# A four-block transformer on one core: gates, shifts and scales spread over the partitions by transfers through memory instead of matmuls, and a bias added by the vector engine

## The chip, the cores and the metric

The kernel runs on one core of a Trainium2 chip. The core has a matrix engine (TensorE, in the profile PE, its weight loads PEld), a vector engine (DVE), a scalar engine (ACT), a general engine (POOL) and SyncE (SP), which here issues nearly all transfers between memory and the 128 partitions of on-chip memory. Every engine works through its own list of instructions in order and waits on semaphores for the others. The metric is the device time of one execution in microseconds; the time of a kernel is the median of several executions.

## The reference

Four blocks follow one another on x, 4 sequences of 512 tokens with 288 channels, in float32. A vector c (4 x 288), one row per sequence, steers each block:

```python
mod = silu(c) @ w_ada + b_ada                       # 4 x 1728
shift0, scale0, gate0, shift1, scale1, gate1 = split(mod, 6)
h = norm(x) * (1 + scale0) + shift0
x = x + gate0 * (attention(h) @ w_proj + b_proj)    # 16 heads of 18
h = norm(x) * (1 + scale1) + shift1
x = x + gate1 * (gelu(h @ w1 + b1) @ w2 + b2)       # 288 -> 1152 -> 288
```

Block 0 replaces the last line by a mixture of experts: four such products, of which each token takes the two with the largest logits, weighted by their softmax. Blocks 0, 1 and 3 attend over the 512 tokens of a sequence; block 2 attends over the 16 heads within each token. A gate, a shift or a scale is a row of 288 numbers that belongs to a whole sequence, so every token of it needs the same row.

## The kernel before, in words

Tokens lie on the partitions in 16 tiles of 128 (TB = 4 tiles are one sequence). The residual x stays on chip. Attention over tokens is written out in steps (L741): per step the score products (L616) of a group of four heads by one tile, the maxima on DVE (L668), exponentials on ACT (L661), and the products with the values (L690). The queries and keys of the next unit of work are computed by L562, copied, and spread by transfers from qc to the qk buffers (L606). Row maxima travel to qk by small transfers (L680).

The order of the work is not left to a scheduler. A small planner inside the program writes it out: `task(where, due, reads, gen)` puts a generator into one of the lists products, lanes, loads and spreads, with a due time counted in gaps and with the names of what it reads. `gap(us)` is called between the matmuls of the main loop and takes pieces from the lists until the given time is filled; `mark(name, delay)` says from which gap on something counts as finished. `other()` hands out the two or so banks of the accumulation memory that the main loop leaves free, in turn. The order in which the planner writes instructions is each engine's order. So moving one task can shift its neighbours. SP's transfers use eight lanes in turn: a transfer is issued only when the one eight before it has landed.

The steering vectors are made by `modulation` and `mod_product` (L348 to L404): matmuls L358 with silu(c) give rows of four partitions, one per sequence, DVE adds the bias (L364), and for most halves PE transposes shifts and scales (L396) so that they lie along the channels. Three things need a row on all 128 partitions:

- `gating(l, half)` (L406): block l's gate, half 0 for attention and half 1 for the MLP. For each of the four sequences a matmul with K=4 (L413) multiplies a 4 x 128 selector, `selb`, with the four rows, and ACT copies the result to the gate tile (L414). There are eight calls.
- `token_modulation(b)` (L420): shift and scale of block 0's experts, for one sequence; two matmuls (L427) and two ACT operations (L428), the second adding 1 to the scale. There are four calls.
- b2, the second bias of an MLP. `mlp()` (L1590) takes whole sequences: block 3's four, and the first of block 1. It starts each accumulation with a matmul with K=1 (L1625), a row of ones with b2, four per call, then L1628 accumulates the second products and `add_gated` (L518) multiplies by the gate on DVE (L522) and adds to x on POOL (L523). `half_mlp()` (L1653) does the same for half sequences with its own matmuls (L1684).

The selector is loaded by three transfers at the start (L1735), between x and the expert router's weights wg (L1736, L1737). The calls of `gating` and `modulation` are queued in the main program:

Of the kernel before, what the change touches and what calls it, by code (L numbers as in the profile page):

```python
# [10 lines left out]
F32 = mybir.dt.float32  # L11
AF = mybir.ActivationFunctionType
ALU = mybir.AluOpType
# [45 lines left out]
def tile_dit_blocks(ctx: ExitStack, tc: tile.TileContext, x_in, cond_t, sel_den, sel_b, w_gate, layers, out):  # L59
# [33 lines left out]

    products, lanes, loads, spreads = [], [], [], []
    open_product, open_lane, open_load, open_spread = [], [], [], []
    WAIT = "wait"
# [201 lines left out]
    def load_mlp(l, e):  # L298
# [5 lines left out]
        for i in range(NF // 3):  # L304
# [97 lines left out]
    def gate_product(l, half):  # L402
        mod_product(l, half, range(2, 3))
        yield 1.5  # L404

    def gating(l, half):  # L406

        row = rows_of[l, half]
        gate = gates[l, half] = wpool.tile([P, B, C], F32, tag=f"gate{half}", name=f"gate_{l}_{half}")
        at = slice(2 * HP, 2 * HP + B)  # L410
        for b in range(B):
            pg = other()
            nc.tensor.matmul(pg[:, :C], selb[at, b, :], row[at, :C], start=True, stop=True)  # L413
            nc.scalar.copy(gate[:, b, :], pg[:, :C])  # L414
            yield 0.5
        mark(("gate", l, half))

    tokens_mod = {}

    def token_modulation(b):  # L420

        row = rows_of[0, 1]
        tokens_mod[b] = [work.tile([P, C], F32, tag="ho", bufs=2, name=f"mod_{k}_{b}") for k in range(2)]
        for kind in range(2):
            at = slice(kind * HP, kind * HP + B)
            pg = other()
            nc.tensor.matmul(pg[:, :C], selb[at, b, :], row[at, :C], start=True, stop=True)  # L427
# [89 lines left out]

    def add_gated(t0, n, pp, gate, name):  # L518

        b = t0 // TB  # L520
        upd = work.tile([P, 2, C], F32, tag="upd", bufs=2, name=f"upd_{name}")
        nc.vector.tensor_tensor(upd[:, :n, :], pp, gate[:, b : b + 1, :].to_broadcast([P, n, C]), ALU.mult)  # L522
        nc.gpsimd.tensor_tensor(x[:, t0 : t0 + n, :], x[:, t0 : t0 + n, :], upd[:, :n, :], ALU.add)  # L523
# [1018 lines left out]
    def experts(base, start):  # L1542
# [3 lines left out]
        for b in range(B):  # L1546
            due = base + 2 * (LEAD + (b + 1) * NG * TB + 14)
            easy = 80 if b < B - 1 else 0
            task(products, due - 12, [("mod", 0, 1)] + ([("xh", 0, 1, b - 1)] if b else []), token_modulation(b))
            task(lanes, due, [("x", 0, 1, b), ("token mod", b)] + ([("scattered", b - 1)] if b else []), norm(0, 1, b))  # L1550
# [39 lines left out]
    def mlp(l, e, b, groups, hook=None, home="ot"):  # L1590
# [30 lines left out]
        def down(fs, hid):  # L1621
            if fs[0] == 0:
                for t in range(TB):
                    r = slice(t * HP, t * HP + 1)
                    nc.tensor.matmul(banks[:, t, :C], ones[r, :], w["b2"][r, :], start=True, stop=False)  # L1625
            for f, hf in zip(fs, hid):
                for t in range(TB):
                    nc.tensor.matmul(  # L1628
                        banks[:, t, :C], hf[:, t * P : (t + 1) * P], w["w2"][f // 3][:, f % 3, :],
                        start=False, stop=f == NF - 1,  # L1630
                    )
# [4 lines left out]
            if fs[-1] == NF - 1:  # L1636
                for i in range(TB // 2):
                    t0 = b * TB + 2 * i
                    add_gated(t0, 2, banks[:, 2 * i : 2 * i + 2, :C], gate, f"m_{l}_{e}_{b}_{i}")
                    if l == n_layers - 1:  # L1640
# [81 lines left out]
    for b in range(B):  # L1722
# [7 lines left out]
        if b == 2:  # L1730
            for g in range(1, NG):
                w_att[0]["load unit"](g, nc.sync)
            load_modulation(0, 0, range(2, 3))
    for kind in range(3):
        nc.sync.dma_start(selb[kind * HP : kind * HP + B], sel_b)  # L1735
    nc.sync.dma_start(wg[:, :KF, :], w_gate[: KF * P, :].rearrange("(k p) e -> p k e", p=P))  # L1736
# [4 lines left out]
    for l in range(n_layers):  # L1741
# [204 lines left out]
```

## Time and profile before

| | us |
| --- | --- |
| median of 3 executions (2443.11 to 2450.07) | 2448.73 |
| the profiled execution | 2468.24 |
| its span, first to last instruction | 2466.5 |
| PE busy | 2282.2 |
| DVE busy | 1069.5 |
| ACT busy | 832.8 |
| POOL busy | 527.1 |
| mean granted PE clock, share of full speed | 0.941 |

A row of a timeline gives the start, the busy time, the engine, the line of the program, the operation, what it writes and reads, the shape and the number of records in the row; brackets hold the idle time of the engine before the row and what ended it. A float32 matmul has two records on PE. "SPq" is SP's queue of transfers. The row PEclk of the page gives the granted clock of PE in 40 equal slices of the span, in tenths of full speed. The profiled execution is slower than the median by 19.5 us, so differences of a few microseconds between two profiles are to be read stage by stage.

### The profile page before, as it was taken

What the parts mean: (1) busy time and instruction counts of PE and PEld (TensorE: products, weight loads), DVE (VectorE), ACT (ScalarE), POOL (GpSimd) and SP (SyncE); (2) the same over time, 40 slices, a digit from 0 to 9 for tenths busy, and PEclk for the clock granted to TensorE, in tenths of its full rate; (3) what the DMA queues carried; (4) which work ended last, traced back from release to release, by engine and by line L of the source; (5) the groups of instructions that cost most, each with busy time, mean ns of one, the idle gap of its engine ahead of it and who ended that gap; (6) DMA issues with size and microseconds to landing.
All of it is one profiled execution on the core that took longest, in us unless ns stands there. A gap on an engine that the chain in (4) does not pass through costs nothing.

```text
span 2466.5 us, 30142 instructions
## 1 busy us (share of the span) xinstructions
PE 2282.2 (93%) x11188; PEld 1204.9 (49%) x11188; DVE 1069.5 (43%) x1944; ACT 832.8 (34%) x1233; POOL 527.1 (21%) x555
## 2 busy tenths in 40 slices
PE   5999999799998999899998999877799999999998
PEld 2233333257775674333353477655467433333455
DVE  3455665432021014555516457898510455555100
ACT  1344434422221222444425333332233344445311
POOL 2000020221021021100001157888621000001000
PEclk8799999899999998999999999888799799999999
DMA  3221121445553552000100000211110000000000
GB/s 80 70 82 39 44 69 39 106 142 178 174 180 113 169 172 76 15 15 14 31 23 1 23 3 8 59 20 20 33 45 7 22 16 17 15 13 7 1 19 20
DMA packets 163032, 134.22 MB, mean 54 GB/s; under 512 B 81365, under 2 KB 146725, under 8 KB 162886
## 3 DMA queue, kind: packets, MB, share of 16 engines
q1 hardware_dynamic: 159520, 122.39, 17.2%
q0 software_dynamic: 3072, 9.44, 1.2%
q8 instruction: 89, 1.46, 0.2%
q10 hardware_dynamic: 294, 0.47, 0.1%
q14 instruction: 57, 0.47, 0.1%
HBM read 90.67 MB, written 26.25 MB: 47 GB/s over the span
## 4 chain that ended last, share of the span: by engine, by line
PE 80%; DVE 5%; DMA 4%; POOL 3%; ACT 2%; issue 2%; SPq 2%; another core or an unknown queue 0%; ACTq 0%; POOLq 0%; DVEq 0%
PE banks L616 19%; PE banks L562 10%; PE banks L690 7%; PE banks L1477 6%; PE banks L1457 6%; PE banks L727 4%; PE banks L1687 4%; PE banks L1665 4%; PE banks L1628 4%; PE banks L1601 3%; PE banks L840 2%; DMA qk<-qc 2%; POOL pv L876 2%; PE banks L1672 1%; PE banks L508 1%
## 5 line engine op out<-in xcount | busy, mean ns | idle before, releaser
L668 DVE TENSOR_REDUCE mx<-banks 128x1 f32<-128x512 f32 x696 | 448.0, 685 | 373.4 <-PE banks L616 370.6
L616 PE MATMUL banks<-qk 32*128 32x512 f32 x3072 | 548.5, 678 | 26.2 <-DMA qk<-qc 13.6
L661 ACT ACTIVATE ex<-banks 128x1024 f32<-128x1024 f32 x348 | 356.4, 1024 | 511.0 <-PE banks L616 506.9
L616 PEld LDWEIGHTS banks<-qk 32*128 32x128 f32 x3072 | 176.6, 193 | 245.0 <-DVE mx L668 96.5
L690 PE MATMUL banks<-ex,va 128*32 128x512 f32 x1536 | 213.2, 626 | 0.0
L562 PE MATMUL banks<-ht,wqk 96*128 96x512 f32 (+1 forms) x360 | 195.1, 649 | 8.7 <-POOL wqk L284 8.1
L876 POOL TENSOR_TENSOR pv<-hs,qk 128x1152 f32<-128x1152 f32 x60 | 190.1, 3182 | 23.3 <-ACT hs L1017 23.3
L1477 PE MATMUL banks<-w_b,hid_b 128*128 128x288 f32 x684 | 188.2, 417 | 0.0
L1457 PE MATMUL banks<-block,w_b 128*128 128x256 f32 x684 | 166.0, 388 | 3.8 <-DMA w_b<-in_w 2.8
L710 POOL COPY rec<-r 128x512 f32<-128x512 f32 x48 | 29.6, 617 | 642.8 <-DVE r L706 569.1
L1469 ACT ACTIVATE hid_b<-banks,b_b 128x256 f32<-128x256 f32 x171 | 68.8, 473 | 247.9 <-PE banks L1463 150.8
L1477 PEld LDWEIGHTS banks<-w_b,hid_b 128*128 128x128 f32 x684 | 124.3, 191 | 51.9 <-issue 24.8
L1665 PE MATMUL banks<-ht,w 128*128 128x256 f32 x504 | 131.9, 397 | 18.8 <-ACT hid L1676 18.3
L1457 PEld LDWEIGHTS banks<-block,w_b 128*128 128x128 f32 x684 | 129.6, 194 | 30.0 <-issue 9.2
L1687 PE MATMUL banks<-w,hid 128*128 128x288 f32 x504 | 144.2, 421 | 0.0
L727 PE MATMUL banks<-wp,ot 128*128 128x288 f32 x384 | 120.4, 440 | 5.9 <-DVE upd_a L522 3.5
L1665 PEld LDWEIGHTS banks<-ht,w 128*128 128x128 f32 x504 | 97.3, 198 | 42.7 <-ACT hid L1676 21.5
L523 POOL TENSOR_TENSOR x<-x,upd_a 128x288 f32<-128x288 f32 x48 | 38.1, 794 | 370.5 <-DVE upd_a L522 347.9
L562 PEld LDWEIGHTS banks<-ht,wqk 96*128 96x128 f32 (+1 forms) x360 | 62.1, 194 | 110.3 <-issue 87.6
L1687 PEld LDWEIGHTS banks<-w,hid 128*128 128x128 f32 x504 | 89.4, 189 | 43.0 <-issue 24.7
L727 PEld LDWEIGHTS banks<-wp,ot 128*128 128x128 f32 x384 | 69.2, 196 | 77.1 <-issue 52.6
L690 PEld LDWEIGHTS banks<-ex,va 128*32 128x32 f32 x1536 | 31.2, 110 | 153.2 <-issue 151.5
(226 smaller groups left out, 2564.6 us busy)
## 6 DMA issues: line engine op xcount, KB each, us to landing
w_b<-in_w SPq DMA_DIRECT2D x57, 432.0 KB
w_b<-in_w SPq DMA_DIRECT2D x57, 384.0 KB
qk<-qc SPq DMA_DIRECT2D x327, 38.0 KB
wa<-in_wada SPq DMA_DIRECT2D x7, 864.0 KB
block<-x_mem SPq DMA_DIRECT2D x19, 288.0 KB
y_mem<-y_b SPq DMA_DIRECT2D x19, 288.0 KB
x_mem<-zeros SPq DMA_DIRECT2D x7, 768.0 KB
y_mem<-zeros SPq DMA_DIRECT2D x7, 768.0 KB
```

What stands on the lines that cost most here:

```text
L562: nc.tensor.matmul(to, st(rows, k), mv(rows, k), start=k == 0, stop=k == NK - 1)
L616: nc.tensor.matmul(to, qk[u][r, of, c * P : (c + 1) * P], qk[u][r, 1 - of, :], start=True, stop=True)
L661: nc.scalar.activation(e, WEIGHTS, AF.Exp)
L668: nc.vector.tensor_reduce(mxs[mu % 2][:, mc, h : h + 1], pm[j], AX.X, ALU.max)
L690: nc.tensor.matmul(SUMS[j * HP : (j + 1) * HP, :], vas[0][:, c, at : at + HP], ex[step, j // 2][:, j % 2, :], start=c == 0, stop=c == TB - 1,)
L727: nc.tensor.matmul(pp, done[b * NG + g][:, t * P : (t + 1) * P], w["wp"][:, g, :], start=g == 0, stop=g == NG - 1)
L876: engine.tensor_tensor(prod, sc[i][:, hs, :].unsqueeze(2).to_broadcast([P, GH, HD, NH]), qkv[i][:, 1].rearrange("p h d -> p d h").unsqueez ...
L1457: nc.tensor.matmul(banks[:, UP + j, :BT], w1[:, k, j * P : (j + 1) * P], hx[i][:, k, :], start=k == 0, stop=False)
L1477: nc.tensor.matmul(banks[:, PY + t, :C], hid[j][:, t * P : (t + 1) * P], w2[:, j, :], start=f == 0, stop=f == NF - 1)
L1628: nc.tensor.matmul(banks[:, t, :C], hf[:, t * P : (t + 1) * P], w["w2"][f // 3][:, f % 3, :], start=False, stop=f == NF - 1,)
L1665: nc.tensor.matmul(banks[:, UP + j, :BT], full[:, k, (f % 3) * P : (f % 3 + 1) * P], h[:, k, s], start=k == 0, stop=False,)
L1687: nc.tensor.matmul(banks[:, PY + t, :C], hf[:, t * P : (t + 1) * P], w["w2"][f // 3][:, f % 3, :], start=False, stop=f == NF - 1,)
```

## The change

`gating` no longer uses PE and ACT. It writes its four rows to memory by a transfer, lets four gaps pass, and reads them back by one transfer that gives each of the 128 partitions all four rows (589,824 bytes written on chip). `token_modulation` does the same with one row of shift and one of scale, each written once as four rows and read per sequence; 1 is added to the scale once, by DVE, on the four rows. These tasks stand in a list of their own, `casts`. The first gate waits in the plan for the maxima of unit 2 also. `mlp()` loads b2 onto all partitions by one transfer, and `add_gated` adds it on DVE ahead of the gate. `half_mlp()` is unchanged. The selector and its three loads are gone.

```diff
+        fill(casts, open_cast, 1000.0)
...
-    selb = const.tile([P, B, P], F32, name="selb")
...
-                for r in range(TB):
-                    nc.sync.dma_start(t["b2"][r * HP : r * HP + 1, :], w["b2"][e : e + 1, :])
+                nc.sync.dma_start(t["b2"], w["b2"][e : e + 1, :].to_broadcast([P, C]))
...
         if (l, half) == (0, 1):
-            mark(("mod", l, half), 2)
+            scale = rows_of[l, half][HP : HP + B, :C]
+            nc.vector.tensor_scalar_add(scale, scale, 1.0)
+            yield 1.0
+            tokens_mod["rows"] = [to_memory(rows_of[l, half][k * HP : k * HP + B, :C], f"t{k}") for k in range(2)]
+            mark(("mod", l, half), 6)
             return
...
+    def to_memory(row, name):
+
+        mem = dram.tile([row.shape[0], C], F32, tag="row", bufs=4, name=f"row_mem_{name}")
+        nc.sync.dma_start(mem, row)
+        return mem
+
     def gating(l, half):
-        row = rows_of[l, half]
+        mem = to_memory(rows_of[l, half][2 * HP : 2 * HP + B, :C], f"{l}_{half}")
+        for _ in range(4):
+            yield WAIT
         gate = gates[l, half] = wpool.tile([P, B, C], F32, tag=f"gate{half}", name=f"gate_{l}_{half}")
-        at = slice(2 * HP, 2 * HP + B)
-        for b in range(B):
-            pg = other()
-            nc.tensor.matmul(pg[:, :C], selb[at, b, :], row[at, :C], start=True, stop=True)
-            nc.scalar.copy(gate[:, b, :], pg[:, :C])
-            yield 0.5
-        mark(("gate", l, half))
+        nc.sync.dma_start(
+            gate.rearrange("p b c -> p (b c)"), mem.rearrange("(o b) c -> o (b c)", o=1).to_broadcast([P, B * C])
+        )
+        mark(("gate", l, half), 8)
+        yield 0.0
...
     def token_modulation(b):
         for kind in range(2):
-            at = slice(kind * HP, kind * HP + B)
-            pg = other()
-            nc.tensor.matmul(pg[:, :C], selb[at, b, :], row[at, :C], start=True, stop=True)
-            nc.scalar.activation(tokens_mod[b][kind], pg[:, :C], AF.Copy, bias=float(kind))
-            yield 0.5
-        mark(("token mod", b))
+            nc.sync.dma_start(tokens_mod[b][kind], tokens_mod["rows"][kind][b : b + 1, :].to_broadcast([P, C]))
+        mark(("token mod", b), 8)
+        yield 0.0
...
-    def add_gated(t0, n, pp, gate, name):
+    def add_gated(t0, n, pp, gate, name, bias=None):
+        if bias is not None:
+            nc.vector.tensor_tensor(upd[:, :n, :], pp, bias.unsqueeze(1).to_broadcast([P, n, C]), ALU.add)
+            pp = upd[:, :n, :]
         nc.vector.tensor_tensor(upd[:, :n, :], pp, gate[:, b : b + 1, :].to_broadcast([P, n, C]), ALU.mult)
...
         def down(fs, hid):
-            if fs[0] == 0:
-                for t in range(TB):
-                    r = slice(t * HP, t * HP + 1)
-                    nc.tensor.matmul(banks[:, t, :C], ones[r, :], w["b2"][r, :], start=True, stop=False)
...
-                        start=False, stop=f == NF - 1,
+                        start=f == 0, stop=f == NF - 1,
...
-    for kind in range(3):
-        nc.sync.dma_start(selb[kind * HP : kind * HP + B], sel_b)
...
-        task(products, base + 20, [("gate row", l, 0)] + before, gating(l, 0))
+        task(casts, base + 20, [("gate row", l, 0)] + before + ([("maxima", 0, 2)] if l == 0 else []), gating(l, 0))
...
-        task(products, base + 60, [("gate row", l, 1)] + before, gating(l, 1))
+        task(casts, base + 60, [("gate row", l, 1)] + before, gating(l, 1))
```

In the order that the planner writes, the modulation tasks (1,0), (3,0) and (3,1) come a little later than before, since they wait for a gate's mark; modulation (1,1) comes earlier; and one piece of block 0's key and query products (L562, second sequence, fourth tile group) comes about five steps later.

More of the change, by code (lines that the diff above doesn't have):

```diff
@@ L92, in tile_dit_blocks @@
     ready = {}
-    products, lanes, loads, spreads = [], [], [], []
-    open_product, open_lane, open_load, open_spread = [], [], [], []
+    products, lanes, loads, spreads, casts = [], [], [], [], []
+    open_product, open_lane, open_load, open_spread, open_cast = [], [], [], [], []
     WAIT = "wait"
@@ L404, in gate_product @@
         yield 1.5
+    def to_memory(row, name):
+        mem = dram.tile([row.shape[0], C], F32, tag="row", bufs=4, name=f"row_mem_{name}")
+        nc.sync.dma_start(mem, row)
+        return mem
     def gating(l, half):
-        row = rows_of[l, half]
+        mem = to_memory(rows_of[l, half][2 * HP : 2 * HP + B, :C], f"{l}_{half}")
+        for _ in range(4):
+            yield WAIT
         gate = gates[l, half] = wpool.tile([P, B, C], F32, tag=f"gate{half}", name=f"gate_{l}_{half}")
-        at = slice(2 * HP, 2 * HP + B)
-        for b in range(B):
-            pg = other()
-            nc.tensor.matmul(pg[:, :C], selb[at, b, :], row[at, :C], start=True, stop=True)
-            nc.scalar.copy(gate[:, b, :], pg[:, :C])
-            yield 0.5
-        mark(("gate", l, half))
+        nc.sync.dma_start(
[3 more added lines that the diff above has]
+        yield 0.0
     tokens_mod = {}
     def token_modulation(b):
-        row = rows_of[0, 1]
         tokens_mod[b] = [work.tile([P, C], F32, tag="ho", bufs=2, name=f"mod_{k}_{b}") for k in range(2)]
         for kind in range(2):
-            at = slice(kind * HP, kind * HP + B)
-            pg = other()
-            nc.tensor.matmul(pg[:, :C], selb[at, b, :], row[at, :C], start=True, stop=True)
-            nc.scalar.activation(tokens_mod[b][kind], pg[:, :C], AF.Copy, bias=float(kind))
-            yield 0.5
-        mark(("token mod", b))
+            nc.sync.dma_start(tokens_mod[b][kind], tokens_mod["rows"][kind][b : b + 1, :].to_broadcast([P, C]))
+        mark(("token mod", b), 8)
+        yield 0.0
     xh, ht = {}, {}
@@ L1548, in experts @@
             easy = 80 if b < B - 1 else 0
-            task(products, due - 12, [("mod", 0, 1)] + ([("xh", 0, 1, b - 1)] if b else []), token_modulation(b))
+            task(casts, due - 12, [("mod", 0, 1)] + ([("xh", 0, 1, b - 1)] if b else []), token_modulation(b))
             task(lanes, due, [("x", 0, 1, b), ("token mod", b)] + ([("scattered", b - 1)] if b else []), norm(0, 1, b))
@@ L1638, in down @@
                     t0 = b * TB + 2 * i
-                    add_gated(t0, 2, banks[:, 2 * i : 2 * i + 2, :C], gate, f"m_{l}_{e}_{b}_{i}")
+                    add_gated(t0, 2, banks[:, 2 * i : 2 * i + 2, :C], gate, f"m_{l}_{e}_{b}_{i}", w["b2"])
                     if l == n_layers - 1:
```

## The prediction

> **What bounds the kernel now.** I read the page's first rows, then the chain.
>
> ```profile
> PE 2282.2 (93%) x11188; PEld 1204.9 (49%) x11188; DVE 1069.5 (43%) x1944; ACT 832.8 (34%) x1233; POOL 527.1 (21%) x555
> ...
> PEclk8799999899999998999999999888799799999999
> ...
> PE 80%; DVE 5%; DMA 4%; POOL 3%; ACT 2%; issue 2%; SPq 2%; another core or an unknown queue 0%; ACTq 0%; POOLq 0%; DVEq 0%
> ```
>
> TensorE (PE) is busy 93% of the span and holds 80% of the chain that ended last. So a matmul taken from a stretch where PE has no gaps shortens the end by its length, and one taken from a stretch held by another engine is worth less. The timeline of PE shows which removed matmul lies where. First the start, PE and then SP's queue:
>
> ```profile
> 46.33 2.04 PE L616 MATMUL banks<-qk 32*128 32x512 f32 x2 [12.54 <-DMA qk<-qc]
> 49.44 2.20 PE L616 MATMUL banks<-qk 32*128 32x512 f32 x6 [1.07 <-DMA qk<-qc]
> ...
> 72.84 3.06 PE L413 MATMUL banks<-row,selb 4*128 4x288 f32 x8
> ```
> ```profile
> 31.34 6.82 SPq L1735 DMA_DIRECT2D selb<-in_sel_b  x3
> 38.20 0.57 SPq L1736 DMA_DIRECT2D wg<-in_w_gate  x1
> 38.82 0.46 SPq L1737 DMA_DIRECT2D wg<-in_w_gate  x1
> 39.40 21.55 SPq L606 DMA_DIRECT2D qk<-qc  x13
> ```
>
> PE waits 12.54 us for the first spread of the queries (L606), and SP issues it only after the three selb loads, of which the second waits 6 us for a DMA lane. Then gates inside other work (one matmul is two records):
>
> ```profile
> 119.05 0.51 PE L427 MATMUL banks<-row,selb 4*128 4x288 f32 x1
> 119.06 0.92 PE L616 MATMUL banks<-qk 32*128 32x512 f32 x3
> ...
> 489.53 1.59 PE L427 MATMUL banks<-row,selb 4*128 4x288 f32 x4 [0.25 <-ACT block L1431]
> ...
> 1024.78 1.23 PE L616 MATMUL banks<-qk 32*128 32x512 f32 x3 [3.34 <-DVE mx L668]
> 1024.80 1.32 PE L413 MATMUL banks<-row,selb 4*128 4x288 f32 x2
> ...
> 1403.15 2.47 PE L413 MATMUL banks<-row,selb 4*128 4x288 f32 x8
> ...
> 1581.92 1.36 PE L413 MATMUL banks<-row,selb 4*128 4x288 f32 x4
> 1586.59 2.28 PE L413 MATMUL banks<-row,selb 4*128 4x288 f32 x4 [3.31 <-ACT gate L414]
> ...
> 1835.18 2.52 PE L413 MATMUL banks<-row,selb 4*128 4x288 f32 x8
> ```
>
> The windows by stage show where PE is no bound: from 1600 to 1750 it is busy 108.8 of 150 us, POOL 115.6, DVE 120.1. From 120 to 300 it is busy 176.4 of 180.
>
> **The change part by part**, against the profiled span of 2466.5 us.
>
> *Start.* Without selb, wg's first load issues at 31.3, its second takes the lane wait to 37.5, and the first spreads go out at 38.0 to 39.9 instead of 39.4 to 42.9: 3.0 us. PE then runs without gaps from 49.4, so 3.0 comes through (0 if the spreads wait for lanes anyway, 4 if not at all).
>
> *Gates (L413), eight calls.* Each loses four matmuls. In full-clock stretches without gaps a call is 2.4 to 2.5: (2,0) 2.4, (3,0) 2.4, (1,0) between the rows of 507 and 513 2.4. (0,0) lies at half clock, 3.0. (0,1) and (1,1) are mixed in pairs with L616, which the K=4 matmul overlaps: 2.0 each. (3,1) at 1928 lies in a stretch where L631's maxima on DVE hold PE: 1.0 (0 to 2.5). (2,1) takes away 3.31 of idle and 3.3 of matmuls, but in front of the stretch that POOL and DVE hold: 3.3 (0 to 11.9, below).
>
> The Trainium skill, "TensorE: Matmul & The Clock Gate", Part 1: an idle window of about 3.4 us puts PE at half clock, and as much sustained work gives full clock back. The first half agrees with the 3.31 us row. The second doesn't: the window 1584 to 1607 has clock 0.50 for 23 us with PE 17.2 busy. By the rule the cure would be worth 3.3 + 1.7 = 5.0 us, by the row up to 3.3 + 8.6 = 11.9. I take neither in full, since POOL is busy 18.7 and DVE 20.0 of those 23 us: PE's slowness is mostly hidden there.
>
> *Token modulation (L427), four calls.* By the periods of the neighbouring L616 rows a matmul costs 0.43 to 0.48, not its 0.9 of busy: six in the first three calls (b = 0 to 2) 2.9; the last call 1.5 at half clock. 4.4.
>
> *Moves.* modulation(1,1) (L358, L364, L396) comes earlier. Its POOL copies (L366) stand ahead of the scatter of b=2 in POOL's order, and in the trace the scatter starts at 518.5 although its places are ready at 508.4; about 3 us earlier then. An idle of 2.89 us before L396 at 530.6 goes or shrinks. I take 2.0 (-1 to 4). qc of b=1, m=4 (L562) moves five steps of 5.2 us later; its spread needs a qk buffer that is free only two steps before the move ends and is used five steps after (26 us, of which nine transfers take up to 18): 8 us of margin, so nothing.
>
> *b2 (L1625), five calls.* The page has 40 records of 0.40, 16 us. But the group of L1628 with them has a period of 12.72 us, without them 12.23: [...] 0.49 x 5 = 2.4.
>
> *What is added.* DVE: ten adds like this row of the tail, 0.76 each:
>
> ```profile
> 2456.82 0.76 DVE L522 TENSOR_TENSOR upd_m<-banks,gate 128x576 f32<-128x576 f32 x1 [29.04 <-PE banks L1628]
> 2457.66 2.75 POOL L523 TENSOR_TENSOR x<-x,upd_m 128x576 f32<-128x576 f32 x2 [28.00 <-DVE upd_m L522]
> 2457.79 0.76 DVE L522 TENSOR_TENSOR upd_m<-banks,gate 128x576 f32<-128x576 f32 x1 [0.21 <-PE banks L1628]
> ```
>
> At the very end the order is add, multiply, add, multiply, so POOL's second L523 starts after four operations instead of two; POOL's first hides part: +1.1. In layer 1's early call the add precedes waiting L616 products: +0.8. The other calls hide it: DVE is idle 28 us before them; bare, they would cost 1.5 each. DVE's scale+1 (one 4x288) hides behind the maxima.
>
> *Transfers*, all in SP's order, eight DMA lanes in turn: 8 writes and 8 broadcasts of 576 KB (gates), 2 writes and 8 broadcasts of 144 KB (token modulation); less 3 selb and 9 of b2. An issue occupies SP 0.25 to 0.6. A write must have landed before its broadcast issues. The trace has no 576 KB broadcast; the nearest rows are rows<-scratch (L906, 576 KB) landing after 3.9 to 4.8, and b_b<-in_b (L1416, one row to 128 partitions, 144 KB) after 2.3 to 4.8. So 4 to 19 (four times the slower), I take 5, nearest to the equal size. The skill speaks against this part: "DMA: Bandwidth & Descriptors", section "Anatomy of one DMA": each transfer has about 2 us of fixed cost, mostly the write's receipt, heaviest towards HBM. By it the round trip costs at least 4; the trace says more, 5.3 to 7.9 for scratch<-ho (L902, to memory) plus 4.8, some 11. Either would be lost if anything waited. But SP's next urgent issues are further off: after gate (0,0), (1,0), (1,1), (3,1), these are due about 9, 12, 11 and 12 us after the broadcast issues (an estimate: gate (1,1) can issue near 1041, since its write follows POOL's combine that ends at 1027, and the next maxima issue near 1052; gate (1,0) near 527, w1's products start at 539); the other gates have 20 and more; the gates themselves are read tens of us later. The waiting instruction is SP's broadcast (for its write), and behind it in SP's order stand: at (0,0) the zeros of x_mem (768 KB) and unit 2's or 3's maxima; at (1,0) the next expert's w1; at (1,1) and (3,1) the next maxima (L680); at token modulation b=0, with gate (0,1), the spread of unit 4, issued at 118 to 124 and used near 150. In attention the write before qk's third spread puts eight instead of six of its nine issues behind the 864 KB wa load's lane, +1.3 us, against 27 us until its products. So 0.
>
> *ACT* loses 40 copies, off the path but for (2,1).
>
> *Sum:* 3.0 + gates (3.0 + 2.0 + 2.4 + 2.0 + 2.4 + 3.3 + 2.4 + 1.0 = 18.5) + 4.4 + 2.0 + 2.4 = 30.3; less 1.9 = 28.4. The profiled execution goes from 2468.2 to about 2440. It lies 19.5 above the median; the same microseconds off the median give 2448.7 - 28.4 = **2420**. Its own range, with low and high ends mixed: 2406 to 2436.
>
> **Rivals.**
> - *More than the sum.* With the stall at 1583 the 23 us of half clock go, and other stalls move off the edge of the clock: +8.6 there, 3 more at 530, and one half-clock stretch of 10 us (as at 1024 to 1034, 4.6 in excess): -45, 2404. For it: PEclk is at 7 and 8 in ten slices. Against: POOL and DVE hold 1600 to 1750.
> - *It doesn't do what it says.* The short K=4 and K=1 matmuls lie beside others in the array, as b2's do, and only start and the solid runs at 72, 489, 1403 and 1835 count (3.0 + 3.0 + 1.5 + 4.8 - 1.9 = 10.4): 2438; with the start hidden too, 2441. Against: the L413 rows at 1403 and 1835 are blocks of eight with nothing in between.
> - *Slower.* One memory row read by 128 partitions is slow, 19 us. Then what SP issues next is late by 10, 7, 8 and 7 us at the four gates named, and each stall brings half clock, 4.6 in excess as at 1024: 32 + 18 = 50, less 28: +22, 2471. From about 13 us per broadcast it decides. For it: 128 reads of one row in one memory. Against: the b_b row.
>
> **How the numbers follow.** Forecast 0.66, more 0.12, little 0.09, slower 0.13. This kernel's measurement tells about 0.3%, 7.3 us: faster is below 2441.4. The forecast and the larger gain are faster, 0.78; with the upper half of "little", 0.80; same 0.08; slower 0.12. The range leaves out most of "slower" and the tip of "more": 2404 to 2445.
>
> **What would show it.** PE with 120 records fewer than 11188 (64 of L413, 16 of L427, 40 of L1625) and busy about 26 us less than 2282.2 (gates 18.5 less the 3.3 of idle, 4.4, 2.4, and some 4 that lay beside L616); first L616 near 43; no idle near 1583; gate<- broadcasts landing in 4 to 6 us; no new wait of L616 on qk<-qc or qk<-maxima; a tail one microsecond longer. The prediction is wrong if L616 or L1457 shows new idle ended by DMA above 5 us, or if the half-clock stretches shift: one more of 23 us costs up to 9.

## The result

The changed kernel takes 2428.6 us (median of 7 executions, 2424.1 to 2436.3), the kernel before 2448.7 (7 executions beside it, 2442.7 to 2456.7). The ratio is 0.9917, 95% interval 0.9898 to 0.9937: 20 us faster, where 28 were forecast. A second set of executions on another occasion (run e8_after) gave the same ratio, 0.9917 (0.9900 to 0.9935). The profiled execution took 2431.8 us, its span is 2430.1.

The page of the changed kernel, the rows that answer to those shown of before:

```profile
PE 2234.5 (92%) x11068; PEld 1186.2 (49%) x11068; DVE 1079.8 (44%) x1955; ACT 818.6 (34%) x1193; POOL 527.0 (22%) x555
...
PEclk8999999899999998999999999897899799999999
...
PE 78%; DVE 6%; DMA 5%; POOL 4%; SPq 3%; ACT 2%; issue 2%; POOLq 0%; ACTq 0%; DVEq 0%
```

PE has the 120 records less that were counted, and is still the bound. Lines have moved: L616 is now L624, L1628 is L1632.

The first profile of the kernel before was a long execution (2468 us), so its difference of 36 us to the one above isn't the change's worth. I profiled the kernel before a second time (run e9_before, 2442.8 us, a short one) and cut the three spans at the same matmuls. Windows of that second profile of before; the columns are the stretch and its length, busy time of PE, PEld, DVE, ACT and POOL with their instructions, granted PE clock, DMA share and GB/s:

```profile
59.14:111.66 52.52, 50.24 (x212) 17.04 (x212) 26.05 (x43) 18.09 (x27) 1.42 (x2) 0.83 0.25 80
111.66:281.65 169.99, 166.36 (x1005) 60.02 (x1001) 98.70 (x183) 78.91 (x92) 8.48 (x14) 1.00 0.16 58
281.65:441.31 159.66, 153.54 (x902) 58.88 (x901) 102.25 (x253) 70.43 (x84) 32.79 (x53) 1.00 0.17 55
441.31:516.74 75.43, 60.31 (x291) 36.20 (x288) 20.84 (x96) 20.42 (x38) 15.43 (x28) 0.84 0.49 142
...
1254.56:1414.55 159.99, 146.27 (x734) 78.47 (x733) 84.22 (x143) 61.95 (x86) 31.01 (x33) 0.95 0.03 10
...
1544.59:1614.58 69.99, 54.44 (x203) 35.76 (x201) 62.71 (x78) 21.94 (x40) 62.64 (x44) 0.77 0.13 23
...
1764.61:1824.61 60.00, 59.94 (x264) 41.22 (x263) 6.19 (x19) 22.63 (x45) 13.03 (x20) 1.00 0.15 46
```

The same stretches of work in the changed kernel:

```profile
60.77:110.47 49.70, 42.98 (x192) 13.82 (x194) 26.97 (x46) 15.07 (x18) 1.42 (x2) 0.93 0.38 103
110.47:282.39 171.92, 167.26 (x1002) 61.69 (x999) 98.10 (x182) 78.55 (x90) 8.82 (x14) 1.00 0.18 62
282.39:447.75 165.36, 157.33 (x894) 58.26 (x893) 102.45 (x253) 68.91 (x80) 32.70 (x53) 0.97 0.17 55
447.75:516.00 68.25, 53.75 (x279) 34.04 (x276) 20.38 (x96) 18.23 (x32) 15.43 (x28) 0.85 0.58 169
...
1251.96:1407.60 155.64, 139.86 (x726) 75.77 (x725) 86.89 (x145) 60.44 (x82) 31.48 (x33) 0.96 0.04 14
...
1537.60:1606.67 69.07, 47.00 (x195) 32.88 (x193) 63.44 (x79) 20.80 (x36) 63.54 (x44) 0.83 0.15 33
...
1757.37:1814.72 57.35, 57.35 (x256) 39.99 (x255) 6.19 (x19) 21.05 (x41) 13.03 (x20) 1.00 0.18 59
```

The stretches where the clock stays at 1.00 have the same length in every profile of one kernel to 0.1 us, so this comparison is sharp there. It shows at once that the third stretch, with token modulation in it, became 5.7 us *longer*, and that where PE got lighter in the sixth (54.4 to 47.0 busy) the stretch became only 0.9 shorter. The table sets the prediction's terms beside it. "Before" is the second profile and, for the first rows, where the clock differs from execution to execution, also the first profile and that of run e3_bias, which is the kernel before up to the middle; "after" is the two profiles of the changed kernel.

| stage of the first profile (us) | what the sum held there | forecast | measured |
| --- | --- | --- | --- |
| 0 to 60 | start | -3.0 | PE's wait 12.54 to 12.18: -0.4 |
| 60 to 120 | gates (0,0), (0,1), token b=0 | -5.9 | 52.5 to 60.0 becomes 47.2 and 49.7: about -8, between -3 and -13, nearly all of it clock |
| 120 to 290 | nothing | 0 | +1.9 (0.9 of PE work in another order, with less beside it, and 1.1 of idle; e1_gates has it too) |
| 290 to 460 | token b=1, b=2 | -1.9 | 159.7 becomes 163.7 and 165.4: +4 to +6 |
| 460 to 540 | token b=3, gate (1,0), the moves | -5.9 | -7.3 |
| 1000 to 1050 | gate (1,1) | -2.0 | -0.8 |
| 1050 to 1280 | b2 of the first call | -0.5 | -0.5 |
| 1280 to 1440 | gate (2,0), the early call's adds | -1.6 | -4.4 |
| 1570 to 1640 | gate (2,1) | -3.3 | -0.9 |
| 1790 to 1850 | gate (3,0) | -2.4 | -2.7 |
| 1850 to 1960 | gate (3,1) | -1.0 | -0.6 |
| 2280 to the end | b2, four calls, and the tail | -0.9 | +0.1 |

The stages left out together give about -1, and with them the measured column sums to some -20, as the medians do.

The start, first PE and then SP's queue of the changed kernel:

```profile
48.10 2.04 PE L624 MATMUL banks<-qk 32*128 32x512 f32 x2 [12.18 <-DMA qk<-qc]
```
```profile
30.43 0.38 SPq L1738 DMA_DIRECT2D wg<-in_w_gate  x1
39.69 0.33 SPq L1739 DMA_DIRECT2D wg<-in_w_gate  x1
40.14 22.52 SPq L614 DMA_DIRECT2D qk<-qc  x13
```

The wait for a lane that selb's second load had is now wg's second load's, as forecast, and the first spread is issued 0.5 us after the lane comes free and not 2. Yet PE waits 12.18 us and not 9.5. (In this execution the start as a whole is 2 us late, from the loads ahead.)

The end of the changed kernel:

```profile
2418.26 0.76 DVE L528 TENSOR_TENSOR upd_m<-banks,b 128x576 f32<-128x576 f32 x1 [26.63 <-PE banks L1632]
2419.05 0.76 DVE L530 TENSOR_TENSOR upd_m<-upd_m,gate 128x576 f32<-128x576 f32 x1
2419.73 0.75 DVE L528 TENSOR_TENSOR upd_m<-banks,b 128x576 f32<-128x576 f32 x1
2419.96 1.40 POOL L531 TENSOR_TENSOR x<-x,upd_m 128x576 f32<-128x576 f32 x1 [26.85 <-DVE upd_m L530]
2420.51 1.45 DVE L530 TENSOR_TENSOR upd_m<-upd_m,gate 128x576 f32<-128x576 f32 x1
2422.11 1.40 POOL L531 TENSOR_TENSOR x<-x,upd_m 128x576 f32<-128x576 f32 x1 [0.76 <-DVE upd_m L530]
```

Four operations stand on DVE as expected; the last multiply, which now reads upd and no longer the accumulation banks, takes 1.45 and not 0.76 while POOL's add runs; the first one takes 0.76 with POOL at rest.

### The profile page after: what moved, and what is told of

It is laid out like the page before. It is cut to its first block, busy times and chain, and to the rows that moved or that the text cites. A ratio compares the mean times of both kernels' runs of the same rounds, so it can differ in the third digit from the quotient of the medians.

```text
span 2430.1 us, 29899 instructions
## 1 busy us (share of the span) xinstructions
PE 2234.5 (92%) x11068; PEld 1186.2 (49%) x11068; DVE 1079.8 (44%) x1955; ACT 818.6 (34%) x1193; POOL 527.0 (22%) x555
## 4 chain that ended last, share of the span: by engine, by line
PE 78%; DVE 6%; DMA 5%; POOL 4%; SPq 3%; ACT 2%; issue 2%; POOLq 0%; ACTq 0%; DVEq 0%
PE banks L624 19%; PE banks L570 9%; PE banks L698 7%; PE banks L1485 7%; PE banks L1465 6%; PE banks L735 4%; PE banks L1691 4%; PE banks L1669 4%; PE banks L1632 4%; PE banks L1609 3%; POOL pv L884 2%; DMA qk<-qc 2%; PE banks L848 2%; PE banks L1676 1%; DVE mx L676 1%
## 5 line engine op out<-in xcount | busy, mean ns | idle before, releaser
L624 PE MATMUL banks<-qk 32*128 32x512 f32 x3072 | 540.2, 668 | 30.3 <-DMA qk<-qc 13.2
L624 PEld LDWEIGHTS banks<-qk 32*128 32x128 f32 x3072 | 174.5, 190 | 256.4 <-DVE mx L676 101.7
L1691 PEld LDWEIGHTS banks<-w,hid 128*128 128x128 f32 x504 | 90.6, 191 | 43.6 <-issue 24.7
L735 PEld LDWEIGHTS banks<-wp,ot 128*128 128x128 f32 x384 | 67.9, 193 | 77.9 <-issue 54.4
```

The lines of the kernel that those rows point to most:

```text
L624: nc.tensor.matmul(to, qk[u][r, of, c * P : (c + 1) * P], qk[u][r, 1 - of, :], start=True, stop=True)
L735: nc.tensor.matmul(pp, done[b * NG + g][:, t * P : (t + 1) * P], w["wp"][:, g, :], start=g == 0, stop=g == NG - 1)
L1691: nc.tensor.matmul(banks[:, PY + t, :C], hf[:, t * P : (t + 1) * P], w["w2"][f // 3][:, f % 3, :], start=False, stop=f == NF - 1,)
```

## The experiments

My theory after the result: the removed lengths are as read, but PE's clock and the waits that the short matmuls used to fill decide as much as the lengths do. The rivals: lengths alone, and a payback through SP's queue. To weigh the clock I use PE's busy time times (1 - granted clock), summed over windows of one microsecond, and call it the excess over full speed: 107.7 and 88.5 us in the two profiles of before, 76.1 and 74.2 in the two of after.

### The three parts alone (e1_gates, e2_tokens, e3_bias)

Each is the kernel before with one part of the diff. e1_gates:

```diff
-            nc.tensor.matmul(pg[:, :C], selb[at, b, :], row[at, :C], start=True, stop=True)
-            nc.scalar.copy(gate[:, b, :], pg[:, :C])
+        nc.sync.dma_start(
+            gate.rearrange("p b c -> p (b c)"), mem.rearrange("(o b) c -> o (b c)", o=1).to_broadcast([P, B * C])
+        )
```

> The kernel before with only the eight gates moved to transfers through memory (selector and its loads kept for the token modulation). Theory by the sum: the removed L413 matmuls give about 18 us and modulation moves may give 2 more, none of the 3.0 of the start: 2428 to 2432 if the sum's terms hold, and L624-type waits on qk transfers stay as before. Rival, the clock: half-clock stretches fall differently, so the time lies up to 12 us away from that either way, while the full-clock stretches show only the matmuls' own lengths. Rival, payback: if SP's queue pays back, a new wait of the score products on DMA appears and the time is above 2438.

Measured: 2437.1 (7 executions), ratio 0.9954 (0.9938 to 0.9970), 11 us faster, less than the sum's 18 or 20.

e2_tokens:

```diff
-            nc.tensor.matmul(pg[:, :C], selb[at, b, :], row[at, :C], start=True, stop=True)
-            nc.scalar.activation(tokens_mod[b][kind], pg[:, :C], AF.Copy, bias=float(kind))
+            nc.sync.dma_start(tokens_mod[b][kind], tokens_mod["rows"][kind][b : b + 1, :].to_broadcast([P, C]))
```

> The kernel before with only the token modulation moved to transfers through memory. Theory by the sum: 4.4 us, so about 2444. Rival, the clock: within 3 us of before or past 8 us, with the difference in half-clock stretches. Rival, payback: slower than before, with qk spreads late after 118 us.

Measured: 2455.9 (14 executions), ratio 1.0024 (1.0011 to 1.0036): slower by 6 to 7.5 us, where a gain of 4.4 was expected. The theory of lengths falls for this part. It was run again later as e12_tokens:

> The kernel with only the token modulation through memory once more, unaltered, beside the one before it in the list (K=4 against K=128) on the same chip. 2454 to 2458 if the first measurement holds, with the half-clock stretch near 492 to 514 again.

Measured: 2453.1 (12 executions), ratio 1.0013 (0.9995 to 1.0030): slower or equal, no gain.

It is lost at two places. The first: the stage of token modulation b=1 and b=2 (290 to 460) is 159.7 us long in e1_gates, in e3_bias and in the second profile of before, which keep L427, and 163.7 to 165.5 in ten profiles of kernels without it. (The first profile of before is the exception: 170.0, with 8.5 of excess there.) Around token modulation b=2, the timeline of the second profile of before:

```profile
389.05 0.66 PE L717 MATMUL banks<-ident,rec 128*128 128x128 f32 x4
389.64 0.51 PE L427 MATMUL banks<-row,selb 4*128 4x288 f32 x1
...
390.23 1.02 PE L616 MATMUL banks<-qk 32*128 32x512 f32 x3
391.75 1.69 PE L616 MATMUL banks<-qk 32*128 32x512 f32 x4 [0.51 <-DMA qk<-maxima]
393.38 1.06 PE L690 MATMUL banks<-ex,va 128*32 128x512 f32 x8
```

and of the changed kernel:

```profile
392.41 0.66 PE L725 MATMUL banks<-ident,rec 128*128 128x128 f32 x4
393.00 1.37 PE L624 MATMUL banks<-qk 32*128 32x512 f32 x4
395.12 1.82 PE L624 MATMUL banks<-qk 32*128 32x512 f32 x4 [0.75 <-DMA qk<-maxima]
396.87 1.94 PE L698 MATMUL banks<-ex,va 128*32 128x512 f32 x8
```

PE reaches the wait for the row maxima sooner, since L427 no longer stands in front of it; the wait grows from 0.51 to 0.75 us, and the next products run at half speed (1.94 us for 1.06). The maxima themselves are not later: the products behind the wait start 2.70 us after the row of L717 (391.75 and 389.05) and 2.71 after that of L725 (395.12 and 392.41), so the broadcasts that now share SP's queue didn't hold them up here. The two or three such stretches cost 3.4 to 5.1 us of excess, and idle grows by 1.9, against 1.3 us of matmuls saved. That the longer wait sets off the half clock is read from the order of these rows and not shown: no run changed the wait alone, the first profile of before had half clock after a wait of 0.50 at 405.6 too, and longer waits in the same stage (1.94 us in the second profile of before, 1.77 in the changed kernel) were not followed by it, though one of 1.78 in e2_tokens was.

The second place: from 460 to 540, where gate (1,0) still stands as K=4 matmuls, e2_tokens takes 80.8 us and e12_tokens 82.5, for 75.4 in the second profile of before; excess is 14.2 and 15.2 for 7.6. The section on e11_gate128 comes back to it.

e3_bias:

```diff
-                    nc.tensor.matmul(banks[:, t, :C], ones[r, :], w["b2"][r, :], start=True, stop=False)
+            nc.vector.tensor_tensor(upd[:, :n, :], pp, bias.unsqueeze(1).to_broadcast([P, n, C]), ALU.add)
```

> The kernel before with only b2 added by DVE in the whole-sequence MLPs. Theory by the sum: 2.4 gained, 1.9 given back: 0.5 us, 2448. By the matmuls' busy time (16 us) it would be 2435. If the tail costs more than 1.1 (the profile of the changed kernel suggests 2.1), 2449; the order of PE is otherwise untouched, so every full-clock stretch ahead of 1260 us must agree to 0.1 us and any difference there is the clock alone.

Measured: 2451.2 (14 executions), ratio 1.0008 (0.9994 to 1.0022): no difference, as expected. Per call PE comes 0.48 to 0.52 us earlier; from PE's last matmul to the end it is 1.7 us longer (10.51 for 8.86).

### The selector's loads put back (e4_selb)

```diff
+    for kind in range(3):
+        nc.sync.dma_start(selb[kind * HP : kind * HP + B], sel_b)
```

> The changed kernel with the three selector loads put back at their place (the tile is loaded and not used). Theory by the sum: 3.0 us slower than the changed kernel, 2431 to 2432, with the first spreads issued some 1.5 to 3 us later after the lane's release. Rival: the start is held by the lane and the landing of the spread, the loads only fill the wait: equal to the changed kernel, 2428 to 2429.

Measured: 2433.6 (6 executions), ratio 0.9927 (0.9908 to 0.9947), which the time can't tell from the changed kernel (the median lies 3 to 5 us above that kernel's two, the intervals overlap). The trace can: PE's wait is 12.55 us with the loads and 12.18 without, 0.4 and not 3.0. The landings say why. In the first profile of before four spreads issued at 39.4, 41.3, 42.0 and 42.9 land at 44.6, 46.2, 47.8 and 49.3; in the second profile of the changed kernel four spreads issued at 38.3, 39.0, 39.6 and 40.3 land at 44.5, 46.1, 47.6 and 49.2. Spreads land one every 1.55 us, whenever they are issued: earlier issue only makes the flight longer (6.3 to 8.9 us and not 4.9 to 6.4). From the release of the lane to the first landing it is 7.0 us in both profiles of before and 6.7 in both of the changed kernel, although the first spread is issued 1.4 us sooner after that release. The rival holds; what sets the first landing stays open.

### Extra matmuls: K=4 against K=128 (e5_k4, e6_k128)

The changed kernel, with 32 matmuls that nobody reads at the places where the gates' stood. K is the number of rows (partitions) over which a matmul sums, of 128. Both kernels have the same order on PE and differ in K alone:

```diff
+        task(products, base + 20, [("gate row", l, 0)] + before, extra_products(l, 0))
...
+        at = slice(2 * HP, 2 * HP + B)
...
+            nc.tensor.matmul(pg[:, :C], ident[at, :], extra[at, :], start=True, stop=True)
```

In the second kernel `at` is slice(0, P), all 128 rows.

> The changed kernel with 32 extra matmuls at the eight places in the plan where the gates' matmuls stood, K=4 like those, of the same length, on constants; nobody reads them and no copy follows. Theory of lengths: they cost what the sum took for the gates, 15 to 18 us, so about 2445, with as much PE time at half clock as in the changed kernel (76 us in excess of full speed in its profile). Rival, the clock counts rows: matmuls that use 4 of 128 rows look like idleness to PE's clock gate, so excess at half clock rises by 10 to 20 and the time is about 2455, at or above the kernel before.

> The same as the run before it, in the same order on every engine, with K=128 in place of K=4. Theory of lengths: the same 2445, or up to 3 more because K=128 can't lie beside the 32-row score products. Rival, the clock counts rows: excess at half clock stays at 70 to 80, the time is 2443 to 2448 and lies 8 or more under the run with K=4.

Measured: with K=4 2453.4 (12 executions), ratio to before 1.0019 (1.0001 to 1.0038); with K=128 2443.0 (7 executions), 0.9958 (0.9940 to 0.9977). One record lasts 0.40 us in both. The 10 us between them aren't length: excess is 93.2 with K=4, 78.5 with K=128, and the mean granted clock of every execution is 0.939 to 0.951 with K=4 (12 executions) and 0.952 to 0.957 with K=128 (7). The stage of the first two gates (60 to 120), with K=4:

```profile
58.86:118.76 59.90, 57.08 (x210) 18.46 (x210) 26.64 (x45) 15.06 (x18) 1.42 (x2) 0.72 0.29 86
```

and with K=128:

```profile
58.84:112.40 53.56, 50.75 (x209) 17.27 (x210) 27.17 (x46) 15.09 (x18) 1.42 (x2) 0.84 0.25 80
```

These two rows alone prove little, since this stage ran from 52 to 60 us in profiles of one kernel, the one before; the times and the clocks of all executions carry the reading. So a matmul on 4 of 128 rows costs its length and, in this stream, a lower clock besides. (K=4 also lay beside other matmuls more: the work that it adds over run e8_after, busy less excess, is 12 us, with K=128 16.)

### The gates on PE, but with K=128 (e11_gate128)

e2_tokens, its 32 gate matmuls made K=128 by a selector that is zero outside four rows:

```diff
-            nc.tensor.matmul(pg[:, :C], selb[at, b, :], row[at, :C], start=True, stop=True)
+            nc.tensor.matmul(pg[:, :C], selb[:, b, :], row[:, :C], start=True, stop=True)
```

> The kernel with only the token modulation through memory and the gates by matmuls, but those 32 matmuls with K=128 in place of K=4: the selector is zero outside its four rows and the rows' tile is cleared before it is filled (nine short DVE memsets more, two selector loads fewer); order on PE the same. If PE's clock counts rows: 8 to 12 us less than the same kernel with K=4, some 2445, and no half-clock stretch of 20 us at the first expert block near 490 to 515. Rival, lengths alone: 2455 to 2458, K=128 not being shorter.

Measured: 2438.2 (6 executions), ratio 0.9948 (0.9931 to 0.9965), against 2453.1 for e12_tokens on the same chip: 15 us, by filling rows with zeros. The mean granted clock is 0.952 to 0.959 in these 6 executions, 0.941 to 0.949 in the 12 of e12_tokens. Gate (1,0) in e12_tokens, timeline and then windows:

```profile
501.55 1.13 PE L1464 MATMUL banks<-block,w_b 128*128 128x256 f32 x4 [0.55 <-ACT hid_b L1476]
502.61 0.86 PE L424 MATMUL banks<-row,selb 4*128 4x288 f32 x2
503.39 2.08 PE L1464 MATMUL banks<-block,w_b 128*128 128x256 f32 x4
505.40 1.32 PE L424 MATMUL banks<-row,selb 4*128 4x288 f32 x2
```
```profile
502.00:524.00 22.00, 22.00 (x64) 10.94 (x63) 4.55 (x22) 2.92 (x8) 2.71 (x6) 0.53 0.15 49
```

and in e11_gate128:

```profile
488.79 1.13 PE L1467 MATMUL banks<-block,w_b 128*128 128x256 f32 x4 [0.55 <-ACT hid_b L1479]
489.75 0.65 PE L427 MATMUL banks<-row,selb 128*128 128x288 f32 x2
490.24 1.03 PE L1467 MATMUL banks<-block,w_b 128*128 128x256 f32 x4
```
```profile
480.00:502.00 22.00, 21.45 (x116) 15.37 (x115) 8.61 (x39) 4.00 (x10) 5.52 (x9) 1.00 0.21 67
```

With K=4 the clock is 1.00 up to 503 and 0.50 from 504 to 523: it falls during the first K=4 row, and from 504 to 523 PE is busy for all 19.00 us. With K=128 it stays at 1.00 after the same wait of 0.55. The whole stage, first in e12_tokens, then in e11_gate128:

```profile
457.89:540.39 82.50, 66.58 (x287) 38.60 (x284) 20.62 (x96) 19.70 (x36) 15.44 (x28) 0.77 0.47 138
```
```profile
445.79:516.87 71.08, 56.93 (x287) 35.70 (x284) 21.46 (x98) 19.80 (x36) 15.43 (x28) 0.86 0.53 156
```

It isn't certain each time: both profiles of the kernel with only the token part have this stretch (that of e12_tokens is one of its longer executions, 2466.5 us, that of e2_tokens, 2455.1, is not), but in the two profiles of before and in e3_bias the same K=4 gate at this place ran at full clock.

### Broadcasts four times as long (e10_slow)

```diff
+        for _ in range(4):
             nc.sync.dma_start(
                 gate.rearrange("p b c -> p (b c)"), mem.rearrange("(o b) c -> o (b c)", o=1).to_broadcast([P, B * C])
             )
```

> The changed kernel with each of the eight gate broadcasts issued four times over, so that a gate is there, and what stands behind it on SP goes out, as late as with a broadcast of about 17 to 19 us. Theory of the sum (slack behind the gates about 9 to 12 us): a stall of 5 to 10 us at one to four places, 2440 to 2465; if SP doesn't wait between equal broadcasts, only the bandwidth counts and it is 2428 to 2433. The rival forecast as slower: 2471 or more. If nothing waits at all, 2428, and the slack was larger than I took.

Measured: 2470.4 (4 executions), ratio 1.0083 (1.0068 to 1.0098): 40 us more than the changed kernel (2430.5 and 2428.6). SP's queue and PE's waits:

```profile
106.56 12.15 SPq L422 DMA_DIRECT2D gate<-row_mem  x4
...
150.76 17.30 SPq L422 DMA_DIRECT2D gate<-row_mem  x4
```
```profile
135.41 5.28 PE L625 MATMUL banks<-qk 32*128 32x512 f32 x12 [9.21 <-ACT ex L670]
...
174.96 1.19 PE L625 MATMUL banks<-qk 32*128 32x512 f32 x1 [5.69 <-DMA qk<-maxima]
...
1067.75 2.14 PE L625 MATMUL banks<-qk 32*128 32x512 f32 x4 [3.02 <-DMA qk<-maxima]
```

SP stands for 12 and 17 us, and the maxima and spreads behind it are late. By stages: 120 to 290 is 24.7 us longer, 460 to 540 7, 1050 to 1280 6.9, and the others from 120 on are the same. So in the changed kernel the transfers are hidden, but at these places by no more than some ten microseconds: in its first profile a broadcast lands after 3.8 to 4.6 us, twice after 9.6 and 10.2.

### Two repairs, and the changed kernel again (e7_late_tail, e8_after)

```diff
-            tokens_mod["rows"] = [to_memory(rows_of[l, half][k * HP : k * HP + B, :C], f"t{k}") for k in range(2)]
+            mark("token rows", 2)
...
+        task(casts, base + 20, ["token rows", ("maxima", 0, 1)], token_rows())
...
+        last = l == n_layers - 1 and b == B - 1
...
+            if last and fs[0] == 0:
...
+                    nc.tensor.matmul(banks[:, t, :C], ones[r, :], w["b2"][r, :], start=True, stop=False)
```

`token_rows` holds the two writes that were taken out; the call of the last sequence in the last block has no DVE add.

> The changed kernel with two repairs: the two writes of the token modulation's rows stand on SP behind the third unit's spread and the second unit's maxima, not ahead of them; and the very last MLP call takes its b2 by K=1 matmuls again. Theory: in the changed kernel the spread is late by the two writes' lane waits, ACT's copy of maxima waits for its buffer until the spread lands, and the exponentials and PE (3.03 us idle near 97 to 100) wait behind it; so here that idle goes, with up to 3 us of half clock after it, and from PE's last matmul to the end of the span it is 1.5 to 2.2 us shorter against 0.5 more of matmuls. Together 4 to 8 us: 2421 to 2425. Rival: the stall comes from the faster PE alone and returns at the next unit: only the tail's 1 to 1.7, 2427.

> The changed kernel once more, unaltered, for the same chip and a second profile. 2428 if the first measurement holds; the idle of 3.0 near 100 us and the half-clock stretches near 294 and 396 appear again if they belong to the kernel, and not if they are chance.

Measured: 2425.6 (6 executions), ratio 0.9904 (0.9885 to 0.9922), and 2430.5 (5 executions) for the unaltered kernel beside it. The intervals overlap, so that it beats the changed kernel isn't shown by the times. In the traces the tail is as forecast:

```profile
2411.53 0.76 DVE L535 TENSOR_TENSOR upd_m<-banks,gate 128x576 f32<-128x576 f32 x1 [27.12 <-PE banks L1644]
2412.37 2.76 POOL L536 TENSOR_TENSOR x<-x,upd_m 128x576 f32<-128x576 f32 x2 [26.48 <-DVE upd_m L535]
2412.51 0.76 DVE L535 TENSOR_TENSOR upd_m<-banks,gate 128x576 f32<-128x576 f32 x1 [0.21 <-PE banks L1644]
```

From PE's last matmul to the end it is 2.1 us shorter, against 0.5 of matmuls. The other repair proves nothing: the idle of 3.03 us near 100, seen in the first profile of the changed kernel and in e4_selb (3.01), is 0.60 here, but the unaltered kernel's second profile hasn't got it either. My reading of that stall, writes that delay a spread, stays open.

### The kernel before again (e9_before)

> The kernel before, unaltered, for a second profile. Its first one took 2468, 19.5 over the median, with 107.7 us of PE time in excess of full speed. Theory: the stages at full clock have the same lengths to 0.1 us, and only half-clock stretches differ; a run near 2446 has about 85 us of excess. Rival: the difference lies in waits instead.

Measured: 2442.8 (one execution). Cut at the same matmuls, the stages from 120 to 290 and from 1000 on agree with the first profile to 0.1 us. The 25 us between the two lie at 60 to 120 (7.5), 290 to 460 (10.3), 460 to 540 (4.6) and 540 to 1000 (2.2), and 19 of them are excess at half clock. Excess is 88.5, as expected; PE's idle time differs by 4.6 us in all, 3.1 of it from 460 to 540.

## Why the prediction was right, and where its steps were wrong

The sign, the size within a factor and the range were right, but the 20 us are made otherwise than the sum said. Between two short profiles, e9_before and e8_after, the span fell by 18.9 us: PE's work (busy less excess) by 16.7, its excess by 14.3, while its idle time grew by 12.2. The sum had 22 us of work go (26 of busy time, some 4 of it beside other matmuls) at an unchanged clock, and some 6 of idle time (3.0 + 3.3 + 2.0 less 1.9). So it is in part luck that the total came near: less work went than forecast, idle time grew where it was to shrink, and a gain at the clock that was not in the sum covered the gap.

- **Lengths of the gates, right where PE is alone.** (3,0) gave 2.7 for 2.4, b2 0.5 a call for 0.49, the first call's stage exactly. Where the K=4 matmuls lay between score products they were worth less: (1,1) 0.8 for 2.0. PE's busy time fell from 2261.3 in the second profile of before to 2234.5 and 2230.3, 27 and 31 us, where 26 were forecast, but this agreement is luck: 12 to 14 of it is excess, and work fell by 14 to 17.
- **"3.0 comes through" at the start: wrong.** SP did issue sooner, but the first spread landed 6.7 us after the lane's release and not 7.0, and the others follow one every 1.55 us. I took the queue's time as the bound and didn't look at the landings, which the trace of before shows. It was 0.4, near the other end that I had named, "0 if the spreads wait anyway".
- **Token modulation, 2.9 for the first three calls: wrong in sign for b=1 and b=2.** I took what the neighbours' period showed. But after L427 PE stands in a wait, so removing it gains nothing and makes the wait longer; with half clock and 1.9 us more idle the stage is 4 to 6 us longer. L427 hid a wait.
- **Gate (2,1), 3.3: 0.9.** In the changed kernel PE stands there for one wait, 11.61 us, for xh, which ACT writes when POOL's work on the tokens is done (the chain that ended last runs through POOL from 1543.8 to 1562.0):

```profile
1562.65 2.01 PE L513 MATMUL banks<-ident,xh 128*96 128x128 f32 x4 [11.61 <-ACT xh L470]
```

  The weighing of the clock rule was right to leave out the 8.6: excess in this stage did fall (12.3 to 7.3) and work by 2.4, and idle took 6.5 of it back.
- **Tail +1.1 and early call +0.8: 2.1 and 1.9.** I hadn't foreseen that the last multiply lengthens while POOL works (1.45 for 0.76); up to the end of POOL's last add the tail is 1.7 longer. In the early call the score products' wait is longer; in the changed kernel and in e1_gates, which leaves b2 on PE:

```profile
1278.09 2.08 PE L624 MATMUL banks<-qk 32*128 32x512 f32 x6 [5.10 <-DVE mx L676]
```
```profile
1276.78 2.08 PE L623 MATMUL banks<-qk 32*128 32x512 f32 x6 [3.66 <-DVE mx L675]
```

- **Moves, 2.0: not shown.** The stage from 460 to 540 gave 7.3 for 5.9 (busy time 6.6 less, idle 0.6), but the idle of 2.89 before L396, from which the 2.0 were read, belongs to the first profile of before: the second hasn't got it, with the same order of instructions.
- **Transfers, 0: right.** rows<-scratch was the right row for most broadcasts: 3.8 to 4.6 us in the first profile, but 9.6 and 10.2 for (0,1) and (1,1), beyond the 4 to 6 that were to show it. A gate's write took 1.5 to 7.3 us, and write and broadcast together 6.5 to 11.9. The section of the skill that the prediction names for the 2 us describes transfers that GpSimd issues, and these are SP's; its "at least 4" held, and the 11 read from the trace was nearer. The rival "slower" was wrong in its premise (19 us) and right in its mechanism: with four broadcasts for one, e10_slow has stalls at (0,0), (1,0) and (1,1) as named, none at (3,1), and one at (0,1) that I hadn't named. That it came to 2470.4, where the rival said 2471, is luck: the rival set 32 us of waits and 18 of clock against a gain of 28; e10_slow has 20 to 24 us more idle and 22 to 24 more excess than the two profiles of the changed kernel, 40 us in the medians, against a gain of 20.
- **The clock, taken as unchanged: wrong, and this made up for the rest.** Excess fell by 12 to 14 us between the second profile of before and those of after, at 60 to 120, 460 to 540, 1280 to 1440 and 1570 to 1640, where gates had stood. At 60 to 120 it is nearly everything: of the windows' 7.3 us less of busy time 5.9 are excess, and work fell by 1.3, not by the 5.9 of the sum. That K=4 matmuls cost clock is shown by two pairs that differ in K (10 and 15 us). The rival "more" had the effect, but laid it to the wait at 1583.

The Trainium skill, "TensorE: Matmul & The Clock Gate", Part 1, lets the clock fall after an idle window of about 3.4 us. The runs go further: in e12_tokens it fell in the middle of work, after a wait of 0.55 and with 12.45 of the 13 us from 490 to 503 busy. By that rule the stretch from 502 to 524 would cost nothing at half clock; its excess is 10.3 us (22.00 busy at 0.53). The prediction's reading that the 3.31 us row of gate (2,1) agrees with the rule was wrong too: the granted clock of the first profile of before is 0.97 from 1580 to 1584 and 0.50 from 1584 to 1588, so it fell at about 1583.8, half a microsecond into the wait that began at 1583.3. Nor does the prediction's window from 1584 to 1607 speak against the rule's second half, which asks for sustained work, since PE was busy 17.2 of 23 us there; the 19.00 us of e12_tokens without a gap do.

What stays open: why the same K=4 gate at (1,0) brings half clock in one kernel and not in another, and whether the longer wait alone starts it at token modulation. The three parts don't add: alone they gave -11, +2 to +7 and nothing clear of noise, together -20. Some 5 to 7 us of that are seen: the token part alone leaves gate (1,0) on PE as K=4 matmuls, which ran at half clock there; the rest isn't explained.

## What to carry to other kernels

Before counting a removed instruction as gain, look at what its engine meets next: if that is a wait for another engine or a transfer, the instruction was filling it, and the gain can be nothing or less. A transfer that is issued earlier helps only if it also lands earlier, so read the landings of a whole burst before the issue times. And where PE's clock isn't at 1.00 throughout, matmuls on a few rows can cost more than their length: take them off PE or pad them with zeros to all rows, and try both, since padding the gates alone gave 15 us here.

## What the runs showed of the hardware that I had not expected

- Matmuls with K=4 lower PE's clock: 32 of them, against 32 of the same length with K=128, cost 10 us in one pair of kernels (2453.4 and 2443.0) and 15 in another (2453.1 and 2438.2), with mean granted clocks that don't overlap (up to 0.951 and from 0.952; up to 0.949 and from 0.952). In one such stretch PE stood at half clock for 19 us without any idle.
- Spreads of 32 rows from on-chip memory to on-chip memory land 1.55 us apart at the start, for issues 0.6 to 1.9 us apart.
- In stretches at full clock two executions of one kernel agree to 0.1 us over hundreds of microseconds; 19 of the 25 us between two executions of the kernel before were excess at half clock.
